# Pinning the four streams of a forward DFT block on TensorE, and spreading the first group's inverses over more rounds

## The chip, the cores and the metric

The kernel runs on one core of one Trainium2 chip. The metric is the device time of a run in microseconds. Before the change the median of three runs is 3327.26 us (3324.58 to 3335.72). The profiled execution has a span of 3324.8 us. In the text, TensorE is PE (and PEld for its weight loads), VectorE is DVE, ScalarE is ACT, GpSimd is POOL, and SP is SyncE, which only issues transfers here.

## The reference

The input `x` is 32 images of 32 channels, each 128 x 128, in 32-bit floats. Two layers with a residual connection follow each other:

```python
x = x + matrix_sqrt(group_norm(x))       # five Newton-Schulz iterations on every 128x128 matrix
d = real(fft2(group_norm(x)))            # per channel
top = einsum('bixy,ioxy->boxy', d[:, :, :32, :32], weights1)
bot = einsum('bixy,ioxy->boxy', d[:, :, -32:, :32], weights2)
x = x + real(ifft2(zeros with top and bot put back))
```

The first layer computes for each of the 1024 matrices an iteration made of 128 x 128 matrix products. The second layer is a spectral convolution: a forward transform of which 64 x 32 modes are kept, a product over the channels at each mode, and an inverse transform.

## The kernel before, in words

**First layer.** A work item is a group of four channels of one image, 256 items in all. The generator `newton` (with `quartic`) takes an item through 12 yields; each step is one to two sets of four 128 x 128 products or transposes on TensorE into one PSUM bank (`products` L250, `transposed` L256), evicted by VectorE (`plus` L244) or ScalarE (`taken` L236). Four items are under way at once, in four lanes. `prep` computes an image's statistics with bn_stats (L178) from tiles `xs`, loaded two ahead on SP's queue, one tile of four channels per step. `settle` stores the result to the scratch tensor `mid` in DRAM, folds it for the transform on GpSimd (`fold`, L342), and takes statistics again.

**Second layer, forward.** After every second pair of folds, `forward` transforms 16 channels: two fold tiles of 8 channels each meet the cosine and the sine table. Each of the four streams has 128 rows of contraction and only 32 output rows, and they write the four 32-row parts of one PSUM bank (L358 cosine, L360 sine), so that they use four different column groups of TensorE. Two short matmuls (L366, 8 columns) fill a column that the sine streams leave out. ScalarE copies the bank out as `sw` (L370). There are two such blocks in an image, 64 in all. `spectrum` does the other axis (L390), applies the second normalisation and stores the image's spectrum in `xs0` to `xs2` in DRAM.

**Second layer, products and inverses.** The images form groups of 24, 6 and 2. When all spectra of a group are there, `wide_products` (group of 24) or `small_products` (6 and 2) multiplies over channels, mode by mode. Then `inverse` runs for each image of the group: loads of `ob` and of `mid` into `yt`, then two halves, each with a set of 32 small matmuls (L621) and two pairs of 64x512 matmuls (L639), an add on VectorE (L644) and the store to `out` (L600), which is issued one step late.

**What sets the order.** A loop written by hand goes round by round. In each round it advances each lane by one step and, between the lanes, advances one entry of each queue: `preps` after lane 1, `specs` after lane 2, `posts` (settle, forward) after lane 3, `prods` after lane 0, and `backs` (the inverses) after lanes 0 and 2. Once no lane has work (`tail`), every queue advances after every lane. The program order that results is then given to a scheduler, which may move an instruction ahead of others on its engine when it estimates that its inputs are ready sooner. `kept` is `tc.keep_in_program_order`: it holds an instruction behind everything that was traced before it on its engine, by an edge without a semaphore. The matmuls of `forward` were not kept before.

Of the kernel before, what the change touches and what calls it, by code (L numbers as in the profile page):

```python
# [59 lines left out]
def conv_preact_kernel(  # L60
# [8 lines left out]
    nc = tc.nc  # L69
# [4 lines left out]
    tab = const.tile([P, T_COLS], F32, name="tab")  # L74
# [44 lines left out]
    tail = False  # L119
    turn = [0]  # L120

    def bank(pool=None):
        if pool is None:
            pool = ps_ax
            if tail:
                turn[0] += 1
                pool = (ps_ax, ps_ns)[turn[0] % 2]
        return pool.tile([P, 4, P], F32, tag="ps", name="ps")
# [32 lines left out]
    kept = tc.keep_in_program_order  # L161
# [91 lines left out]
    def transposed(t, pool=None):  # L253
        ps = bank(pool)
        for j in range(4):
            nc.tensor.transpose(ps[:, j, :], t[:, j, :], ident)  # L256
        return ps
# [49 lines left out]
    def newton(g, sn, xt, m, mb, r):  # L307


        q = yield from quartic(m, mb, r)  # L310
        y = taken(products(q, m), "y")
        yield
        m = taken(products(q, y), "m", 3)
        yield
        mb = taken(transposed(m, ps_ns), "mb", 2, QR * QS)
        r = four("r", 4)
        nc.gpsimd.tensor_tensor(r, mb, eye, ALU.add)  # L317
        yield
        q = yield from quartic(m, mb, r)
        pw, py = products(q, m), products(q, y)  # L320
        w, y = taken(pw, "t", 3), taken(py, "y4", 2)
        yield
        t = plus(products(w, q), -0.5 * EYE / 1.5, eye, "t", 3)
        yield
        ps = products(t, y)
        for j in range(4):
            c = 4 * g + j
            nc.vector.scalar_tensor_tensor(  # L328
                xt[:, j, :], ps[:, j, :], sn[:, c : c + 1], xt[:, j, :], ALU.mult, ALU.add
            )  # L330
        yield
# [17 lines left out]
    def forward(b, q, u):  # L349


        fs = [folds.pop((b, 2 * q + i)) for i in range(2)]
        ps = bank()
        out = ps.rearrange("p j x -> p (j x)").rearrange("p (c h) -> p c h", h=64)
        cos, sin = (slice(T_FW.start + 32 * i, T_FW.start + 32 * i + 32) for i in range(2))
        for i in range(2):
            rows = slice(64 * i, 64 * i + 32)
            nc.tensor.matmul(out[rows], tab[:, cos], fs[i][:, :, 0:64], start=True, stop=True)  # L358
            rows = slice(64 * i + 32, 64 * i + 64)
            nc.tensor.matmul(  # L360
                out[rows, :, 1:64], tab[:, sin], fs[i][:, :, 65:128], start=True, stop=True
            )

        for i in range(2):
            rows = slice(64 * i + 32, 64 * i + 64)
            nc.tensor.matmul(  # L366
                out[rows, :, 0], tab[:, cos], fs[i][:, :, 64], start=True, stop=True
            )
        sw = sp.tile([P, 4, P], F32, tag="sw", name="sw", bufs=2)
        nc.scalar.copy(sw, ps)  # L370
        yield
        ps = transposed(sw)
        for i in range(2):
            c = 8 * q + 4 * i
            nc.scalar.copy(
                u[:, :, :, c : c + 4].rearrange("h s l c -> h (s l) c"),
                ps[:, :, 64 * i : 64 * i + 64].rearrange("h c m -> h m c"),
            )
        yield
# [283 lines left out]
    def step(queue):  # L663
        if queue and next(queue[0], queue) is queue:
            queue.pop(0)
# [12 lines left out]
    def stage():  # L678

        b, g = stages.pop(0)  # L680
        if g == 0:
            while b not in made:
                step(preps)
            if b + 1 < B:
                preps.append(prep(b + 1, made))
        ready.append(staged(b, g, *made[b]))
        if fetches:
            fetch(*fetches.pop(0))

    def end(b, g, xt):  # L690

        if g == 0:
            u = up.tile([P, 2, L, G], F32, tag="u", name=f"u{b}")
            st = small.tile([P, C, 6], F32, tag="b_st", name=f"b_st{b}")
            ended[b] = (u, st)
        u, st = ended[b]
        posts.append(settle(b, g, st, xt))
        if g % 4 == 3:
            posts.append(forward(b, g // 4, u))
        if g == C // 4 - 1:  # L700
            posts.append(last(b, u, st))
# [25 lines left out]
    rounds = 0  # L727
    while todo or any(lanes) or posts or specs or prods or backs:
        tail = not todo and not any(lanes)
        if tail and not posts and not late:  # L730

            phase.close()
            late.append(ctx.enter_context(tc.tile_pool(name="late", bufs=1)))
            for i in range(3):
                late_xks.append(late[0].tile([P, 4 * NB, 64], F32, name=f"xk{i}_late"))
                nc.gpsimd.memset(late_xks[-1], 0.0)
            for kk in range(2, KK):
                late_wts.append(late[0].tile([P, 2, 4, 4, C], F32, name=f"wt{kk}_late"))
                nc.gpsimd.dma_start(out=late_wts[-1], in_=wk[kk])
        for i in range(LANES):  # L740
            if lanes[i] is None and todo and rounds >= 3 * i:
                b, g = todo.pop(0)
                xt = ready[0][0]
                lanes[i] = (b, g, xt, newton(g, made[b][2], *ready.pop(0)))
                if stages:
                    stage()
            if lanes[i] is not None:
                b, g, xt, steps = lanes[i]
                if next(steps, lanes) is lanes:
                    lanes[i] = None  # L750
                    end(b, g, xt)
            if i == 1:
                step(preps)
            if i == 2:
                step(specs)
            if i == 3:
                step(posts)
            if i == 0 or tail:
                step(prods)
            if i in (0, 2) or tail:  # L760
                step(backs)
        rounds += 1

# [61 lines left out]
```

## Time and profile before

| What | Value |
|---|---|
| median time | 3327.26 us |
| TensorE busy | 3209.1 us, 97% of the span |
| VectorE busy | 2271.0 us, 68% |
| GpSimd busy | 1469.1 us, 44% |
| ScalarE busy | 1391.2 us, 42% |
| moved by transfers | 479.64 MB, mean 144 GB/s |
| first matmul of group 0's mode products (L485) | 2250.6 us |
| first matmul of an inverse (L621) | 2416.5 us |
| transfers from 2416 to 2950 us | 266 GB/s, share 0.82 |
| last forward block starts | 3230.21 us |

Busy time sums the recorded durations of an engine's instructions. Matmuls are pipelined and their ends are modelled, so the distance between starts tells more of TensorE than its busy share does. A matmul of 32-bit floats leaves two records, a transpose one; "x8" in a row is thus a set of four products. "PEclk" is the granted clock of TensorE, and the DMA share is the mean busy share of the core's 16 DMA engines. In a list of waits, a row names the engine and line that stood idle, what released it, the sum in us, how often, and the longest. SPq is the queue of transfers that SP issues: a transfer that must wait for its data holds those behind it.

### The profile page before, as it was taken

The page shows a single profiled execution, that of the slowest core. Times are in us where ns is not written, and L with a number is a line of the kernel's source. Part 1 is how long each engine was busy: PE and PEld are TensorE (multiplying, and loading weights), DVE is VectorE, ACT ScalarE, POOL GpSimd, SP SyncE. Part 2 cuts the span into 40 slices and gives each one's busy share as a digit, 9 for nine tenths or more (in the row PEclk, how much of TensorE's full clock was granted, in tenths as well). Part 3 has the DMA queues.
Part 4 walks back from the last instruction along what each step waited for, and adds up shares of the span by engine and source line. Part 5 has one row for each costly group of instructions (what it writes and reads, how often), then busy time and mean ns, then how long its engine had stood idle before and what let it go on. Part 6 is the DMA issues. An engine that isn't in the chain of part 4 may idle for free.

```text
span 3324.8 us, 82819 instructions
## 1 busy us (share of the span) xinstructions
PE 3209.1 (97%) x33216; PEld 2947.1 (89%) x33216; DVE 2271.0 (68%) x6375; ACT 1391.2 (42%) x2865; POOL 1469.1 (44%) x2077
## 2 busy tenths in 40 slices
PE   6999999999999999999999999999999999999994
PEld 5999999999999999999999999999976777789863
DVE  6777777777777777777777777776565666676551
ACT  2444444444444444444444444444433333344321
POOL 4554555554555545545544545554422323334320
PEclk9999999999999999999999999999999999999997
DMA  3233333333322333333333333226698788854786
GB/s 118 96 103 99 103 99 103 99 99 97 95 91 93 96 100 99 102 99 102 99 100 99 99 99 95 91 90 217 214 306 253 260 273 265 265 183 131 235 266 237
DMA packets 273680, 479.64 MB, mean 144 GB/s; under 512 B 83728, under 2 KB 93968, under 8 KB 273296
## 3 DMA queue, kind: packets, MB, share of 16 engines
q1 hardware_dynamic: 195680, 325.95, 30.5%
q10 hardware_dynamic: 75600, 141.07, 13.4%
q0 software_dynamic: 2016, 7.34, 0.6%
q8 instruction: 261, 4.28, 0.5%
q14 instruction: 123, 1.01, 0.1%
HBM read 319.06 MB, written 155.19 MB: 143 GB/s over the span
## 4 chain that ended last, share of the span: by engine, by line
PE 88%; DMA 7%; DVE 3%; issue 1%; SPq 1%; ACT 0%; DVEq 0%; ACTq 0%
PE ps L250 66%; PE ps L256 11%; DMA xs<-in_xt 5%; PE ps L639 3%; PE ps L621 2%; PE ps L358 2%; DVE a_st L178 1%; PE ps L549 1%; DMA yt<-mid 1%; PE ps L390 1%; PE ps L485 1%; PE ps L360 1%; DVE yt L644 1%; DVE xt L328 0%; DMA xs<-spec 0%
## 5 line engine op out<-in xcount | busy, mean ns | idle before, releaser
L342 POOL TENSOR_TENSOR fold<-xt 128x256 f32<-128x256 f32 x512 | 364.6, 731 | 887.4 <-DVE xt L328 805.1
L293 POOL TENSOR_TENSOR r<-b,eye 128x512 f32<-128x512 f32 x256 | 326.1, 1274 | 817.2 <-issue 804.1
L250 PE MATMUL ps<-w,v 128*128 128x128 f32 x4096 | 547.0, 277 | 1.0 <-DVE w L244 0.9
L250 PE MATMUL ps<-y,q 128*128 128x128 f32 x4096 | 545.4, 276 | 0.0
L250 PEld LDWEIGHTS ps<-w,v 128*128 128x128 f32 x4096 | 499.7, 192 | 15.5 <-issue 8.2
L250 PEld LDWEIGHTS ps<-y,q 128*128 128x128 f32 x4096 | 500.0, 192 | 8.4 <-issue 6.8
L236 ACT COPY y<-ps 128x512 f32<-128x512 f32 x512 | 299.9, 586 | 403.5 <-PE ps L250 402.8
L274 POOL TENSOR_SCALAR x<-xt,a_nm,a_sc 128x128 f32<-128x128 f32 x1024 | 445.7, 449 | 21.9 <-DVE a_n L206 20.6
L244 DVE SCALAR_TENSOR_TENSOR w<-ps,r 128x512 f32<-128x512 f32 x512 | 350.2, 686 | 114.8 <-PE ps L256 109.2
L284 ACT ACTIVATE b<-b,a_off,a_scr 128x128 f32<-128x128 f32 x1024 | 422.3, 486 | 1.4 <-DMA b<-in_x 1.3
L244 DVE SCALAR_TENSOR_TENSOR q<-ps,eye 128x512 f32<-128x512 f32 x512 | 349.1, 682 | 54.4 <-PE ps L250 40.0
L178 DVE BATCH_NORM_STATS2 a_st<-xs 128x6 f32<-128x128 f32 x1024 | 228.9, 280 | 190.3 <-DMA xs<-in_xt 189.9
L328 DVE SCALAR_TENSOR_TENSOR xt<-ps,a_t_s,xt 128x128 f32<-128x128 f32 x1024 | 292.9, 342 | 78.0 <-PE ps L250 77.4
L238 ACT ACTIVATE mb<-ps 128x512 f32<-128x512 f32 x256 | 152.9, 597 | 459.3 <-PE ps L256 443.8
L317 POOL TENSOR_TENSOR r<-mb,eye 128x512 f32<-128x512 f32 x256 | 325.5, 1271 | 40.5 <-ACT mb L238 37.0
L256 PE MATMUL ps<-ident,v 128*128 128x128 f32 x2048 | 317.8, 275 | 7.9 <-DVE v L244 7.6
L244 DVE SCALAR_TENSOR_TENSOR v<-ps,m 128x512 f32<-128x512 f32 x256 | 175.8, 687 | 204.2 <-PE ps L250 193.4
L250 PEld LDWEIGHTS ps<-m,q 128*128 128x128 f32 x2048 | 249.8, 192 | 42.3 <-DVE q L244 31.7
L250 PE MATMUL ps<-y,t 128*128 128x128 f32 x2048 | 280.8, 280 | 3.4 <-DVE t L244 3.1
L250 PE MATMUL ps<-x,b 128*128 128x128 f32 x2048 | 277.9, 279 | 5.4 <-POOL x L274 5.4
L250 PE MATMUL ps<-m,q 128*128 128x128 f32 x2048 | 278.7, 279 | 4.5 <-DVE q L244 4.4
L236 ACT COPY m<-ps 128x512 f32<-128x512 f32 x256 | 149.9, 585 | 313.3 <-PE ps L250 309.1
(115 smaller groups left out, 5053.8 us busy)
## 6 DMA issues: line engine op xcount, KB each, us to landing
b<-in_x ACTq DMA_DIRECT2D x256, 256.0 KB, 2.9
xt<-in_xt ACTq DMA_DIRECT2D x256, 256.0 KB, 3.3
xs<-in_xt SPq DMA_DIRECT2D x256, 256.0 KB, 3.2
mid<-xt SPq DMA_DIRECT2D x256, 256.0 KB, 2.0
yt<-mid SPq DMA_DIRECT2D x128, 512.0 KB, 6.6
out<-yt SPq DMA_DIRECT2D x115, 512.0 KB, 5.8
ob<-od SPq DMA_DIRECT2D x64, 256.0 KB, 6.6
plain<-in_wk SPq DMA_DIRECT2D x18, 512.0 KB, 4.2
```

The source lines that it names most:

```text
L178: nc.vector.bn_stats(st[:, 4 * i + c, :], tiles[i][:, c, :])
L236: nc.scalar.copy(t, ps)
L238: nc.scalar.mul(t, ps, f)
L244: nc.vector.scalar_tensor_tensor(s, ps, f, t, ALU.mult, ALU.add)
L250: nc.tensor.matmul(ps[:, j, :], lhsT[:, j, :], rhs[:, j, :], start=True, stop=True)
L256: nc.tensor.transpose(ps[:, j, :], t[:, j, :], ident)
L274: nc.gpsimd.tensor_scalar(m[:, j, :], xt[:, j, :], nm[:, c // 2 : c // 2 + 1], sc[:, c : c + 1], ALU.add, ALU.mult,)
L284: nc.scalar.activation(mb[:, j, :], mb[:, j, :], AF.Identity, bias=off[:, c : c + 1], scale=scr[:, c : c + 1],)
L293: nc.gpsimd.tensor_tensor(r, mb, eye, ALU.add)
L317: nc.gpsimd.tensor_tensor(r, mb, eye, ALU.add)
L328: nc.vector.scalar_tensor_tensor(xt[:, j, :], ps[:, j, :], sn[:, c : c + 1], xt[:, j, :], ALU.mult, ALU.add)
L342: nc.gpsimd.tensor_tensor(f[:, :, 64 * half : 64 * half + 64], xt[:, :, 0:64], xt[:, :, 64:128], op)
```

## The change

It has two parts. In `forward`, the six matmuls of a block are kept in program order on TensorE, so that the scheduler no longer takes a single stream out of the block when its fold is ready before the other's; the order inside the block also changes (the second fold first, sine before cosine). In the loop, `backs` still advances after lane 0 in every round, but after lane 2 only in odd rounds: an average of one and a half steps in a round and not two, until the tail. It is meant to spread the inverses of the first group over the rounds until the next group's products start.

```diff
-        for i in range(2):
+        for i in (1, 0):
+            rows = slice(64 * i + 32, 64 * i + 64)
+            kept(
+                nc.tensor.matmul(
+                    out[rows, :, 1:64], tab[:, sin], fs[i][:, :, 65:128], start=True, stop=True
+                )
+            )
             rows = slice(64 * i, 64 * i + 32)
-            nc.tensor.matmul(out[rows], tab[:, cos], fs[i][:, :, 0:64], start=True, stop=True)
+            kept(
+                nc.tensor.matmul(out[rows], tab[:, cos], fs[i][:, :, 0:64], start=True, stop=True)
+            )
+
+        for i in (1, 0):
             rows = slice(64 * i + 32, 64 * i + 64)
-            nc.tensor.matmul(
-                out[rows, :, 1:64], tab[:, sin], fs[i][:, :, 65:128], start=True, stop=True
-            )
-
-        for i in range(2):
-            rows = slice(64 * i + 32, 64 * i + 64)
-            nc.tensor.matmul(
-                out[rows, :, 0], tab[:, cos], fs[i][:, :, 64], start=True, stop=True
+            kept(
+                nc.tensor.matmul(
+                    out[rows, :, 0], tab[:, cos], fs[i][:, :, 64], start=True, stop=True
+                )
             )
...
-            if i in (0, 2) or tail:
+            if i == 0 or i == 2 and rounds % 2 or tail:
                 step(backs)
```

## The prediction

> **What bounds the kernel now.** I read the busy time of each engine first, then the busy shares of stretches of the span, then TensorE's instructions in order of time, and last the waits inside the stretch that looked different.
>
> ```profile
> PE 3209.1 (97%) x33216; PEld 2947.1 (89%) x33216; DVE 2271.0 (68%) x6375; ACT 1391.2 (42%) x2865; POOL 1469.1 (44%) x2077
> PE   6999999999999999999999999999999999999994
> ```
>
> ```profile
> 1800.00:2000.00 200.00, 199.71 (x1787) 191.93 (x1786) 149.28 (x438) 90.82 (x189) 100.47 (x142) 1.00 0.33 104
> 2416.00:2950.00 534.00, 512.91 (x6218) 394.14 (x6216) 341.42 (x857) 193.33 (x391) 155.39 (x221) 0.98 0.82 266
> ```
>
> The columns of the stretches are PE, PEld, DVE, ACT, POOL, granted clock, DMA share, GB/s. A busy TensorE alone proves little, since ends are modelled. What proves the bound is the pitch, the time from one group's start to the next one's. Through 33 to 2400 us it is nearly constant: four 128x128 products (8 records) take 0.89 us, four transposes 0.44. I took the usual pitch (lower quartile) of each pair of neighbours and summed what lies above: about 1.06 us per 50 us. So up to 2400 us TensorE is the limit and a microsecond taken from it is a microsecond of span. Between 2400 and 2950 us, where group 0's inverses run, the same sum is 53.9 us; less the usual 1.06 x 11 = 12 it leaves 42 us lost, nearly all near 2500-2560, 2690-2740 and 2810-2860.
>
> Two shapes of a forward block stand in the timeline of TensorE (start, us, operation). First four streams together, then one alone and three later:
>
> ```profile
> 101.19 0.60 PE L256 MATMUL ps<-ident,v 128*128 128x128 f32 x4
> 101.72 0.62 PE L358 MATMUL ps<-fold,tab 128*32 128x512 f32 x1
> ...
> 102.75 1.16 PE L250 MATMUL ps<-y,t 128*128 128x128 f32 x8
> ```
>
> ```profile
> 136.81 1.06 PE L250 MATMUL ps<-w,v 128*128 128x128 f32 x8
> 137.80 1.05 PE L358 MATMUL ps<-fold,tab 128*32 128x512 f32 x2
> 138.77 1.16 PE L250 MATMUL ps<-m,q 128*128 128x128 f32 x8
> 139.77 1.06 PE L250 MATMUL ps<-y,q 128*128 128x128 f32 x8
> ...
> 145.56 0.60 PE L256 MATMUL ps<-ident,v 128*128 128x128 f32 x4
> 146.09 0.61 PE L360 MATMUL ps<-fold,tab 128*32 128x504 f32 x1
> ...
> 147.11 1.16 PE L250 MATMUL ps<-y,t 128*128 128x128 f32 x8
> ```
>
> Four streams occupy 102.75 - 101.72 = 1.03 us; three occupy 147.11 - 146.09 = 1.02; one alone 138.77 - 137.80 = 0.97. The number of streams costs nothing, the number of visits does.
>
> In the inverse stretch, the waits (us in all, times, longest) and the transfer of xs (median us to landing, there and in 600-2200 us):
>
> ```profile
> DVE a_st L178 <- DMA xs<-in_xt: 48.6, 23, 4.9
> ```
>
> ```profile
> SPq L600 <- DVE yt L644: 146.5, 39, 10.0
> ```
>
> ```profile
> xs<-in_xt SPq DMA_DIRECT2D x24, 256.0 KB, 7.0
> ```
>
> ```profile
> xs<-in_xt SPq DMA_DIRECT2D x144, 256.0 KB, 3.2
> ```
>
> VectorE stands at bn_stats for data that lands late, and behind it in its queue are the evictions that TensorE needs. At 2508.9 it had waited 3.99 us for xs; the yt add and the v eviction follow it, and TensorE then stands 1.71 us for v.
>
> **What the Trainium skill says.** "TensorEngine Tiling (Array Packing)", Tiling Modes, Key Properties: a change of tiling mode drains the array. The trace agrees: the group ahead of the lone stream has pitch 0.99 instead of 0.89, and the one behind it 1.00. "TensorE: Matmul & The Clock Gate", Part 3 (Packing small matmuls): matmuls in different column groups run at the same time, a few ns apart; here the four streams start within 0.02 us. The same page, Part 1 (Architectural detail): VectorE is strict FIFO, so a late operand holds all behind it; the 3.99 us above is that. "DMA: Bandwidth & Descriptors", "Issuing engines are not separate DMA queues": the issuing queues share 16 DMA engines; here xs lands in 7.0 us at 0.82 share against 3.2 at about 0.3.
>
> **Part 1, the pin.** The instruction order that the scheduler builds shows 25 of the 64 forward blocks split before, and none after; up to about 2400 us nothing else changes order on any engine. The 25 lone streams stand in the trace from 137.8 to 2198.5 us (24) and at 2997.3, all in TensorE-bound time. Each removed visit gives back 0.97 for itself, 0.10 ahead and 0.11 behind, less 0.01 since four streams take 1.03 and not 1.02: 1.17 us. 25 x 1.17 = 29 us. The steady image period of 89.27 us should become 88.1. The edges add no semaphore; they hold the four behind what was traced before them on TensorE. Queued behind them are products of other lanes. A wait would come from the fold of the pair's last group: it ended at 139.9 on GpSimd, the streams that need it started at 146.09, 6 us later, at the place where the pinned block stays. The changed order of sin and cos inside the block I cost at nothing: they run in four column groups at once.
>
> **Part 2, fewer steps.** A lane keeps an item 13 rounds (12 yields and the end), so an image (8 items, 4 lanes) takes 26 rounds of 89.27 / 26 = 3.43 us. An inverse is 8 steps (7 yields and the end): 4 rounds at two steps a round, 5.33 at one and a half. Group 0's 24 inverses then take 128 rounds instead of 96 (following the loop: rounds 680-808 instead of 680-776). Group 1's products start in round 802 and end at 818, so nothing of group 1 is held up. TensorE's work is the same: per image 2 x (1.16 + 2 x 1.06 + 3 x 0.10) = 7.2 us. What changes is how thick transfers lie. Before, 142 MB in 534 - 42 = 492 us of TensorE work, 289 GB/s asked. After, 32 rounds more of lanes, 110 us at about 100 GB/s: 153 MB in about 600 us, 255 GB/s. An estimate from these: the share falls from 0.82 to somewhat under 0.8, and stores are issued half or a whole round after the add they wait for, not always half, so SP stands less. Against it, the stretch now holds four preparations of an image (every 26 rounds) and not three. Before, one cost 42 / 3 = 14 us. The trace shows no preparation at this load. The bounds are 2 us, near what quiet stretches show, and 14, no better than now; I take 6: 4 x 6 = 24, a gain of 18 us. The ends are +34 and -14.
>
> **Part 3, the end.** Group 1's last two inverses slip: image 29's whole inverse now stands between the last forward block and its spectrum.
>
> ```profile
> 3232.99 0.66 PE L256 MATMUL ps<-ident,sw 128*128 128x128 f32 x4 [1.69 <-ACT sw L370]
> 3234.39 1.64 PE L390 MATMUL ps<-u,tab 64*64 64x256 f32 x16 [0.74 <-ACT u L375]
> ...
> 3262.57 2.09 PE L549 MATMUL ps<-plain,diag 128*32 128x32 f32 x128 [23.62 <-DMA diag<-xs]
> ```
>
> About 2.3 half inverses move behind the last product; earlier that frees 2.3 x 3.6 = 8 us. Between forward and spectrum two halves at the pitch of the end (1.94 + 1.92 each) take 7.7 us where 2.5 us of chain waits now lie empty: +5.2; another 0.3 half ahead: +1.2. Net -2. The 23.6 us wait that follows is transfers (391 to 413 GB/s from 3240 to 3260): image 29's extra 2 to 4 MB at 400 GB/s are 5 to 10 us, beside the 6 us of new TensorE work. I take 0 for the end, bounds -3 and +6.
>
> **Sum.** 3327.3 - 29 - 18 - 0 = 3280.
>
> **The rivals.**
> (A) As summed, 3280: chance 0.50.
> (B) The pin pays, the spreading doesn't: a preparation still costs 10 to 14 us, since xs is two rounds ahead and rounds get shorter along with the landing; 4 x 10.5 = 42, nothing gained: 3298. For it: SP still stands on stores ahead of xs, and demand falls only by an eighth. [...]Chance 0.27.
> (C) Waits for xs nearly vanish, 2 us each: gain 34, end -3: 3327 - 29 - 34 - 3 = 3261. For it: the stretch 2950-3123, without inverses of group 0, loses next to nothing. Chance 0.16.
> (D) Slower: each pinned block waits for its fold or holds ready lanes. With 64 blocks at 1 us and no gain from part 2: 3327 + 64 - 29 = 3362; break-even is 0.45 us a block. Against: the 6 us of slack. Chance 0.03.
> (E) No change: another engine's chain sets the round and TensorE only waits more, 3327. For it: VectorE at 0.75 of the stretch is next. Against: the even pitch. Chance 0.04.
>
> **How the numbers follow.** The range 3260 to 3304 holds A, most of B (up to 14 us per preparation and +6 at the end lie above) and about half of C: 0.50 + 0.22 + 0.08 = 0.80. Faster by over 0.3% (under 3317): A, C and nearly all of B, 0.92. Within 0.3%: E and the rest of B, 0.05. Slower: 0.03.
>
> **What would show it.** Right: L358's group with two records alone is gone, the image period before 2250 us is 88.1, the inverses run about 600 us with DMA share under 0.8, the bn_stats wait for xs falls from 48.6 to some 25 us. Wrong: the period stays 89.3 (E), idle ahead of forward blocks (D), xs waits as long as before (B), or a wait ahead of L549 that grows by over 8 us.

## The result and the profile after

The changed kernel takes 3306.81 us (median of 4, 3304.25 to 3309.52) against 3329.73 us of the kernel before on the same chip: ratio 0.9931, interval [0.9911, 0.9951]. Run again later it gave 0.9925 [0.9913, 0.9938]. It is faster by 23 to 25 us, where 47 were forecast, and lies 3 us above the range.

First the page's busy row of the changed kernel, then two stretches of it (columns as before: PE, PEld, DVE, ACT, POOL, granted clock, DMA share, GB/s).

```profile
PE 3180.5 (96%) x33216; PEld 2940.7 (89%) x33216; DVE 2273.3 (69%) x6375; ACT 1388.5 (42%) x2865; POOL 1474.2 (45%) x2077
```

```profile
1800.00:2000.00 200.00, 199.54 (x1803) 194.39 (x1802) 149.20 (x431) 91.33 (x191) 102.58 (x146) 1.00 0.32 99
2402.00:3000.00 598.00, 580.49 (x6782) 466.63 (x6789) 400.26 (x1031) 227.33 (x466) 201.92 (x288) 0.98 0.75 244
```

TensorE is still busy nearly all the time. Among the inverses the DMA share is 0.75 and not 0.82, at 244 GB/s, close to the 255 that were worked out. The same place of the first image, in the timeline of TensorE:

```profile
136.53 1.06 PE L250 MATMUL ps<-w,v 128*128 128x128 f32 x8
137.82 1.16 PE L250 MATMUL ps<-m,q 128*128 128x128 f32 x8 [0.23 <-DVE q L244]
138.81 1.06 PE L250 MATMUL ps<-y,q 128*128 128x128 f32 x8
...
145.14 0.61 PE L360 MATMUL ps<-fold,tab 128*32 128x504 f32 x1
...
146.16 1.16 PE L250 MATMUL ps<-y,t 128*128 128x128 f32 x8
```

The lone stream is gone and the four streams take 146.16 - 145.14 = 1.02 us. But the products w,v now have a pitch of 137.82 - 136.53 = 1.29 us, where 0.89 is usual, and those behind them 0.99. TensorE stands still exactly where the lone stream used to be. All 24 places before the inverses look the same (pitch 1.28 to 1.29, then 0.99 to 1.00). The new order of sine and cosine shows no price: the four streams took 1.03 before. So a removed visit gave 0.99 + 0.97 + 1.00 less 1.29 + 0.99, which is 0.68 us and not 1.17.

The trace of before had said so, in the weight loads and on VectorE, which the prediction did not read at this place:

```profile
137.80 0.14 PEld L358 LDWEIGHTS ps<-fold,tab 128*32 128x32 f32 x2
138.77 0.97 PEld L250 LDWEIGHTS ps<-m,q 128*128 128x128 f32 x8 [0.84 <-DVE q L244]
```

```profile
137.41 0.63 DVE L244 SCALAR_TENSOR_TENSOR q<-ps,eye 128x512 f32<-128x512 f32 x1
```

The row of the weight loads names q as what they waited for, but its 0.84 us is not the wait for q alone: q ended at 137.41 + 0.63 = 138.04, and the rest is the lone stream. Without that stream the products m,q would have been due at 136.81 + 0.89 = 137.70, 0.34 us before q was there. The stream was cheap because it ran in part while TensorE would have waited. Why q is late is seen on VectorE, here in a later image of the changed kernel (TensorE starts m,q at 1116.83):

```profile
1114.13 0.44 DVE L135 RECIPROCAL a_r_q<-a_r_s 128x48 f32<-128x48 f32 x1
1114.49 0.28 DVE L328 SCALAR_TENSOR_TENSOR xt<-ps,a_t_s,xt 128x128 f32<-128x128 f32 x1
...
1115.79 0.44 DVE L200 RECIPROCAL a_inv<-a_r_s 128x48 f32<-128x48 f32 x1
1116.14 0.63 DVE L244 SCALAR_TENSOR_TENSOR q<-ps,eye 128x512 f32<-128x512 f32 x1
```

Four evictions xt of an item that ends and the root and reciprocal of the next image's preparation come one by one between the last w and q. From 1114.13 to 1116.14 VectorE is busy with them.

The wait of bn_stats for xs from 2390 to 3050 us, and the transfer of xs from 2402 to 3050 us:

```profile
DVE a_st L178 <- DMA xs<-in_xt: 45.9, 20, 7.1
```

```profile
xs<-in_xt SPq DMA_DIRECT2D x32, 256.0 KB, 5.7
```

xs lands in 5.7 us instead of 7.0, yet the wait in all has hardly fallen: before it was 47.1 us from 2416 to 2950, in three preparations of an image, and now it is 45.9 in four. The end, in the timeline of TensorE:

```profile
3196.27 1.23 PE L628 MATMUL ps<-tab,ob 64*32 64x128 f32 x64
3201.33 2.08 PE L646 MATMUL ps<-gt,tab 64*128 64x512 f32 x4 [3.83 <-ACT gt L638]
...
3210.81 1.09 PE L397 MATMUL ps<-u,tab 64*64 64x256 f32 x16
...
3238.36 2.09 PE L556 MATMUL ps<-plain,diag 128*32 128x32 f32 x128 [21.93 <-DMA diag<-xs]
```

From the last product y,t to the spectrum it is 24.4 us and not 12.7. Image 29's inverse lies in between and waits for ScalarE. ScalarE waits 3.69 us at a store for an add, and that add waits 5.81 us for yt:

```profile
3198.93 1.29 DVE L651 TENSOR_TENSOR yt<-ps,yt 128x512 f32<-128x512 f32 x2 [5.81 <-DMA yt<-mid]
3200.69 1.07 ACT L638 COPY gt<-ps 128x512 f32<-128x512 f32 x2 [3.69 <-DVE yt L651]
```

Behind this wait TensorE's granted clock was 0.50, from 3201 to 3207 us.

### The profile page after: what moved, and what is told of

It reads as the page before. It is cut to its first block, busy times and chain, and to the rows that moved or that the text cites. A ratio compares the mean times of both kernels' runs of the same rounds, so it can differ in the third digit from the quotient of the medians.

```text
span 3302.3 us, 82823 instructions
## 1 busy us (share of the span) xinstructions
PE 3180.5 (96%) x33216; PEld 2940.7 (89%) x33216; DVE 2273.3 (69%) x6375; ACT 1388.5 (42%) x2865; POOL 1474.2 (45%) x2077
## 4 chain that ended last, share of the span: by engine, by line
PE 84%; DMA 8%; DVE 6%; issue 1%; SPq 1%; ACT 0%; DVEq 0%; ACTq 0%
PE ps L250 63%; PE ps L256 11%; DMA xs<-in_xt 5%; PE ps L646 3%; PE ps L628 2%; PE ps L360 1%; DVE xt L328 1%; DVE a_st L178 1%; PE ps L556 1%; PE ps L492 1%; PE ps L397 1%; DMA yt<-mid 1%; DMA out<-yt 1%; DVE q L244 1%; DVE yt L651 1%
```

## The experiments

In what follows a kernel's gain is worked out from its ratio to the kernel before, run on the same chip, times 3327 us. Single profiles of one kernel differ by some 4 us in a stretch, so the times decide and profiles show where. The intervals in brackets are those of the ratio; 0.001 is 3.3 us.

**The two parts alone.** The changed kernel with the old line of the loop, and the old kernel with the new one:

```diff
-            if i == 0 or i == 2 and rounds % 2 or tail:
+            if i in (0, 2) or tail:
```

> The pin alone; two inverse steps in every round as before. Theory (bubble): where the lone stream stood, TensorE has to wait for VectorE's q anyway, so a removed visit is worth 0.68 us and not 1.17: 24 x 0.68 + 1 = 17 us below the kernel before, about 3312, first inverse at about 2402. Rival (full price, lost later): 29 us below, about 3300. If the pin also upsets the stretch of inverses, less than 12 us below.

Measured: 3306.87 us, ratio 0.9946 [0.9933, 0.9959], 18 us below; the first inverse starts at 2398.0 us. The interval reaches from 14 to 22 us: it holds the theory's 17 and not the full price of 29, which is refuted.

> One and a half inverse steps a round, no pin. Theory: the spreading gives 12 us back in the stretch of inverses and costs 4.5 us at the end, 7 us below the kernel before, about 3322. Rival: both parts gain only together, and this one alone changes nothing (within 3 us).

Measured: 3318.00 us, ratio 0.9978 [0.9970, 0.9986], 7 us below. The parts add up: 18 + 7 = 25, against the whole change's 23 to 25.

**The wait behind the lone stream.** One more yield in `prep` puts the root one round later. TensorE keeps its order, and four short VectorE operations (not six, as I wrote below) move behind q; of the five between the last w and q only the first reciprocal stays ahead.

```diff
         nc.vector.tensor_scalar(v[:, C:], vg, 0.5, EPS, ALU.mult, ALU.add)
+        yield
         s = root(v, C + G, "a_r")
```

> The changed kernel with one more yield in prep ahead of root, so that six short VectorE operations of the preparation come behind the eviction q that TensorE waits for, with TensorE's order kept. Theory: the wait of 0.4 us ahead of the products m,q in every image vanishes, with the 0.1 us longer pitch behind it: 24 to 30 images x 0.5 = 12 to 15 us below the changed kernel, about 3293, image period 88.4 us. Rival: the wait comes from the length of that lane's chain, not from the preparation: period stays 88.9 and time 3307.

Measured: 3286.19 us, ratio 0.9884 [0.9868, 0.9901], 14 to 16 us below the changed kernel by the ratios. The period is 88.32 us, against 88.93 of the changed kernel and 89.56 of before, each from the first forward block to the 45th. The timeline of TensorE of this kernel, at the same place:

```profile
136.62 1.06 PE L251 MATMUL ps<-w,v 128*128 128x128 f32 x8
137.51 1.06 PE L251 MATMUL ps<-m,q 128*128 128x128 f32 x8
138.40 1.06 PE L251 MATMUL ps<-y,q 128*128 128x128 f32 x8
```

and its VectorE in the same later image, where q follows the four xt at once:

```profile
1106.64 1.05 DVE L329 SCALAR_TENSOR_TENSOR xt<-ps,a_t_s,xt 128x128 f32<-128x128 f32 x4
1107.61 0.68 DVE L245 SCALAR_TENSOR_TENSOR q<-ps,eye 128x512 f32<-128x512 f32 x1
```

Both pitches are 0.89: 0.50 us an image that the pin left behind. Those periods are means, with some slower images in them. From the first block of one image to that of the next, the most frequent distance was 89.25 us before, 88.56 in the changed kernel and 88.07 here: 0.69 and then 0.49 us less. The same yield in the kernel before, with no pin and two steps a round:

> The kernel before with root one round later and neither part of the change. In its instruction order no stream is taken out of a forward block, without any pin. Theory: bubble and visit are two faces of one gap, and the whole price of 1.17 to 1.24 us per image comes back: 24 x 1.24 = 30 us below the kernel before, about 3296. Rival: the pin is needed for the gain: not more than 15 us below.

Measured: 3297.33 us, ratio 0.9908 [0.9894, 0.9922], 31 us below, period 88.42. With the preparation out of the way the scheduler takes no stream out of the 64 blocks, without any pin. Gap and lone stream belong together, and the pin is not needed for the gain.

**The waits for xs.** bn_stats of images 25 to 31 reads the constant tile `eye`; all loads are still issued.

```diff
-                nc.vector.bn_stats(st[:, 4 * i + c, :], tiles[i][:, c, :])
+                nc.vector.bn_stats(st[:, 4 * i + c, :], (eye if b > 24 else tiles[i])[:, c, :])
```

> The kernel before, with bn_stats of the preparations of images 25 to 31 reading a constant tile in place of xs; the xs loads are all issued as before. Left out: the true statistics of seven images. Theory (wait for xs): the loss among the inverses, 33 to 42 us, goes to under 10, about 3293. Rival (adds, stores and thick transfers themselves): less than 10 us, 3318 or more.

Measured: 3294.86 us, ratio 0.9901 [0.9886, 0.9915], 33 us below. The stretch of the inverses in this kernel:

```profile
2416.00:2950.00 534.00, 530.99 (x6538) 418.77 (x6536) 362.08 (x905) 208.81 (x422) 174.66 (x248) 1.00 0.84 279
```

TensorE is busy 531 us of 534 and not 513, and more is moved: 279 GB/s against 266. So it was neither the transfer rate nor the adds that cost 33 us, but VectorE standing at bn_stats, and what followed from it. (The constant tile also takes away what loads of xs waited in SP's queue for a buffer that bn_stats had not yet read, 11.7 us in ten pieces before. This was not tested apart; yt lands in 6.4 us as before.)

What followed from it includes the granted clock, 0.98 in the stretch before and 1.00 here, which the prediction did not take up. In the trace of before it falls to 0.50 in five pieces of 3.4 or 6.8 us, 23.9 us in all, at 2525, 2552, 2699, 2815 and 2842 us, where the losses were found. Each began within 1.6 us of the end of a wait of TensorE of 1.5 to 2.8 us. One of them, as a stretch and in TensorE's timeline:

```profile
2552.20:2558.90 6.70, 6.69 (x58) 4.96 (x66) 3.97 (x7) 0.00 (x0) 0.71 (x1) 0.50 0.74 221
```

```profile
2552.21 2.07 PE L639 MATMUL ps<-gt,tab 64*128 64x512 f32 x2 [1.82 <-DVE yt L644]
2554.21 2.08 PE L250 MATMUL ps<-x,b 128*128 128x128 f32 x8
2556.08 1.92 PE L250 MATMUL ps<-q,t 128*128 128x128 f32 x8
```

The products x,b have a pitch of 1.87 us there, where 0.89 is usual, and all the while TensorE counts as busy. As an estimate from these figures, 23.9 us at half clock cost about 12 us, and the idle time that is gone (21.1 less 3.0 us in the stretch) about 18: together 30 of the 33. With the constant tile no such piece lies among the inverses. The changed kernel has 23.9 us of them too. By what rule the clock falls, no run shows.

> The same constant tile in the changed kernel. Theory (wait for xs): it gains 15 to 20 us, less than the kernel before does, and the spreading is then worth nothing: about 12 us below the other kernel with the constant tile, which is the pin's 17 less the end's 4.5. Rival: the spreading keeps its 7 us: 24 us below.

Measured: 3278.69 us, ratio 0.9851 [0.9835, 0.9867]. That is 25 to 27 us below the changed kernel (0.9925 and 0.9931) and 17 below the other kernel with the constant tile. As the pin alone is worth 18, nothing is left for the spreading when nobody waits for xs; each of these figures has an interval of some 4 to 5 us either way. The sizes between were off: I had expected 15 to 20 and 12. So the spreading seems to work through this wait alone, and took only about 7 of 33 us from it.

**The end.** One and a half steps for group 0 alone (`done0` is filled at the end of group 0's last inverse):

```diff
-            if i == 0 or i == 2 and rounds % 2 or tail:
+            if i == 0 or i == 2 and (rounds % 2 or done0) or tail:
```

> The changed kernel with one and a half steps only until group 0's last inverse has ended; group 1 gets two steps a round again, so that image 29's inverse lies ahead of the last forward block. Theory: the end costs the change 4 to 5 us, so about 3302. Rival: the moved inverse costs earlier what it frees at the end: same as the changed kernel, 3306 to 3307.

Measured: 3302.54 us, ratio 0.9932 [0.9918, 0.9946]; the changed kernel itself has 0.9931 and, in the run below, 0.9925. No difference shows. In the profiles, from the last product to the last matmul it is 93.6 us and not 105.0 (92.9 before the change), but from the first inverse to the last product 792.7 and not 784.1. What the end pays had mostly been freed before, and nothing speaks for my theory of 4 to 5 us.

> The changed kernel once more, on the chip of the others: 0.993 of the kernel before. If the edit for group 0 alone was worth nothing, its ratio of 0.9932 is matched; if it was worth 3 to 5 us, this one lies at 0.994 to 0.995.

Measured: 3302.06 us, ratio 0.9925 [0.9913, 0.9938], which is no higher than the edit's 0.9932. Each interval is some 8 us wide; the next pair points the same way.

> The changed kernel with both edits: root one round later, and one and a half steps for group 0 alone. If the two gains are independent, 20 and 3 to 4 us below the changed kernel, about 3283. Rival: the end's gain vanishes since it was paid ahead of the last forward block: as root later alone, 3286 or above.

Measured: 3291.81 us, ratio 0.9892 [0.9877, 0.9907], no better than root later alone (0.9884). The rival holds; two pairs without a gain make 4 to 5 us unlikely, and a gain of 1 or 2 us can't be excluded.

**A third xs buffer.** As the kernel with both edits, with `stp` of three buffers, three loads ahead, and five `b` buffers.

```diff
-    stp = ctx.enter_context(tc.tile_pool(name="stp", bufs=2))
+    stp = ctx.enter_context(tc.tile_pool(name="stp", bufs=3))
...
-        xt, t = four("xt", 10), four("b", 6)
+        xt, t = four("xt", 10), four("b", 5)
```

> As the kernel with both edits, with three xs buffers and three loads ahead, and five b buffers in place of six to make room. Theory: what is still lost among the inverses is the wait of bn_stats for xs (45 us of VectorE's time): the wait falls below 15 us and the time by 10 to 15 us, to about 3270. Rival: the loads stand in SP's queue behind stores, so depth doesn't help: within 4 us of the kernel with both edits. A tighter b buffer could also cost a few us.

Measured: 3280.23 us, ratio 0.9855 [0.9842, 0.9869], 12 us below the kernel with both edits, but not where the theory put it. Among the inverses bn_stats still waits 31.6 us (41.1 without), not under 15, and the stretch from the first inverse to the last product is no shorter (792.5 us, 788.2 without). The gain lies ahead of them: the first inverse starts at 2380.7 us and not at 2389.9. So depth helps ahead of the inverses, and that a third buffer cures the waits under load is refuted. Of these 9 us, 2 lie ahead of the first forward block already (4 against the control below); most of the rest comes from fewer slow images. The control:

> The kernel with both edits (root later, group 0 alone) and five b buffers, two xs buffers: the control for the kernel with three xs buffers. Theory: the 11 us that three xs buffers brought are theirs, and five b buffers cost nothing: 3288 to 3292, ratio 0.989. Rival: the gain came from the b buffers: ratio 0.9855.

Measured: 3293.82 us, ratio 0.9891 [0.9874, 0.9907]. The five `b` buffers are not the cause.

> The changed kernel with root one round later, three xs buffers and five b buffers, one and a half steps for all groups. Expected from the single edits: 20 plus 9 to 11 us below the changed kernel, 3275 to 3280, ratio 0.985, the lowest of all. Rival: the xs gain was one of the chip's draw: ratio 0.988.

Measured: 3276.64 us, ratio 0.9846 [0.9831, 0.9860], the lowest of all and as expected, 51 us below the kernel before. Its interval overlaps with that of the kernel with both edits and three xs buffers.

## Why the prediction was wrong

**The bound.** The failing step is "up to 2400 us TensorE is the limit and a microsecond taken from it is a microsecond of span". The even pitch had shown that TensorE rarely waited, with the lone streams in place. It did not show that it would not wait without them. At just these 24 places VectorE's q was late: without the lone stream TensorE waits 0.4 us for it, and the pitch after the wait is 0.1 us longer. This took 11 us from part 1. Part 2 fell short by another 11, through the size of one term.

**Part 1, the pin.** The term 25 x 1.17 = 29 us measured 18: 24 x 0.68 = 16 and the visit at 2997. The usual image period, 89.25 us here and 89.27 in the forecast, fell to 88.56 and not to 88.1. The occupation by visits, four streams for the price of one, was right: with the wait gone as well, 31 us came back. That no forward block would wait for its fold was right too.

**Part 2, fewer steps.** The mechanism was right: late xs, VectorE standing in front of evictions, a lower share with fewer steps. The half clock behind TensorE's waits was in the losses that were summed, but not in the account of them. The loss that the changed kernel keeps was forecast at 24 us and measured at 25 to 27; as the 6 us for each preparation had been picked between 2 and 14, this was luck. The mis-sized term is the loss before, taken as 42 us and measured 33: I had subtracted the pitch excess of the quiet part, about 1.06 us per 50, where quiet slices among the inverses show near 2. So 7 us were gained and not 18, inside the bounds given.

**Part 3, the end.** Taken as 0, and the experiment with group 0 alone finds no difference. One of its terms was wrong in size: 11.7 us more from the last product to the spectrum, not 6.4, as loads of yt and the store ahead of ScalarE's copies hold the chain. Behind the spectrum nothing comes back: from the last product to the last matmul it is 105.0 us against 92.9. The work freed before, forecast at 8 us and 8.6 in the profiles, makes up for most of it; what is left is within the differences between profiles.

**The rivals.** The outcome lies between A and E: what E said of the chain of another engine that sets the round was true of some two fifths of the pin's price, 0.49 of 1.17 us, and I had given it 0.04 as all or nothing. B's number, 3298, would have needed the full pin as well.

Left open: which of SP's queue and the transfers themselves makes xs late under load with three buffers, and by what rule the granted clock halves near TensorE's waits.

## What to carry to other kernels

An instruction that a scheduler moved into a gap costs what it adds to the gap, not what it occupies; before its removal is priced, read what the instruction behind it waits for, in the weight loads as well, and when that was done on its own engine. When a gap is found, look at what stands ahead of the awaited operation on the other engine: moving four short operations by one round was worth 31 us in the kernel before, more than both parts of the change, and made the pin needless. A late load was dear here because VectorE waited for it ahead of evictions that TensorE needed. And a busy share hides a halved clock: read the clock of every stretch that is slow.

## What the runs showed of the hardware

Four 32-column streams of 512, with the two short matmuls behind them, took 1.02 to 1.03 us and one alone 0.97. Behind the wait for q the next four products had a pitch of 0.99 to 1.00 and not 0.89, at all 24 places; behind a change of the tile's shape it was 0.99 to 1.00 as well. In pieces of 3.4 or 6.8 us near waits of TensorE the granted clock was 0.50, and four products had a pitch of 1.87 us. Transfers at 279 GB/s and a share of 0.84 left TensorE busy 531 of 534 us once nothing waited in front of evictions.
